# Splits of operands to twelve bits, queued at other places: query rows, output weights, and the first layer's change of rows

## The chip, the cores and the metric

The kernel runs on one core of one Trainium2 chip, in one launch. The metric is the device time of an execution in microseconds (us), as the median of several runs. TensorE is called PE here, VectorE DVE, ScalarE ACT, GpSimd POOL, and SyncE, which issues most DMAs, SP.

## The reference

A graph network on 1024 nodes of width 512: layer norm and relu of the input, batch norm, a graph convolution, four layers of cross-attention and a gated feed-forward net, a second graph convolution, and two additions of the input. Cut to what this change touches, each of the four layers computes:

```python
def _attn(xf, cond, Wq, Wk, Wv, Wo):            # xf 1024x512, cond 16x256x512
    xb = xf.reshape(BS, n // BS, d)             # 16 groups of 64 rows
    q = (xb @ Wq).reshape(BS, -1, H, DH)
    k = (cond @ Wk).reshape(BS, -1, H, DH)
    v = (cond @ Wv).reshape(BS, -1, H, DH)
    att = jnp.einsum('bnhd,bmhd->bhnm', q, k) * DH ** (-0.5)
    w = jax.nn.softmax(att, axis=-1)
    o = jnp.einsum('bhnm,bmhd->bnhd', w, v).reshape(BS, -1, H * DH)
    return (o @ Wo).reshape(n, d)
for i in range(L):                              # L = 4
    h = h + _attn(_ln(h, ln2_w[i], ln2_b[i]), cond, Wq[i], Wk[i], Wv[i], Wo[i])
    u = _ln(h, ln3_w[i], ln3_b[i]) @ geglu_w[i] + geglu_b[i]
    ...
```

## The kernel before

The rows of `h` lie in SBUF as eight blocks of 128 rows; two batches of `cond` make one of eight groups `g`. The large products run on PE in a reduced fp32 form (`twelve_bits`): both operands are split into a high part (ACT, a scaled copy), a low part (DVE) and a third part, a sum or difference of the two (POOL for left operands, DVE for the rows and the output weights). A product is then three sets of four matmuls. The class `Twelve` holds one such product: `begin` multiplies the high parts and the low parts into a PSUM bank and lets ACT scale the bank in place (line 377); `end` multiplies the third parts onto it and copies the bank out. `staggered` runs a list of them so that the `begin` of one stands ahead of the `end` of the one before, with a callback beside each.

A layer begins with the query phase. The rows of `h` are normalised (`xn`), transposed on PE (`tr_ln`, line 201), scaled and shifted out of PSUM into `ln2T` by DVE (line 812) and ACT (line 814) in turn, and split: `Rows.high` makes the high part `bh_ln` on ACT (line 1252), `Rows.rest` makes the low part `bl_ln` (line 1257) and the third part `bs_ln` (line 1260) on DVE. `QueryWeights` does the like for `Wq` (`ah_wq`, `al_wq`, `as_wq`). The queries of the first four blocks are multiplied while the other four are turned and split; then those of the second half follow. In layers 1 to 3 the query phase stands behind the keys and values of group 0; in layer 0 most of these have been made during the graph convolution.

Then come the scores of group 0 and the loop over the groups: the keys of the next group, the weighing of the values of this one (`po`), the scores and the softmax of the next group (DVE line 834 takes the maxima `nmax`, ACT line 839 eight exponentials `pr`, DVE line 844 divides), the values of the next group, and the product with the output weights `wo`. `out_parts` splits `wo` once a layer, in group 0: `oh` on ACT (line 915), `ol` and `os` on DVE (lines 918 and 921). `split_cond` splits the `cond` of the group after next (`ah_c`, `al_c`, `as_c`; lines 314, 315 and 320). In groups 1 and 2 `base_of` prepares two blocks of the final sum from the input `x`: a load `x_again`, an ACT operation `again` (line 1526), two DVE additions (1528 and 1529), and a store (1530).

What order the instructions of an engine get is decided by the scheduler of the language, except where the code pins it: `pin` keeps the written order, `in_order(engine)` chains all that is recorded inside it on that engine, `waiting_for` adds a wait. PE's large products are pinned. In layers 1 to 3 ACT and parts of DVE are chained in the query phase; in layer 0 they are not. `base_of` and the copies around the softmax are nowhere pinned.

Of the kernel before, what the change touches and what calls it, by code (L numbers as in the profile page):

```python
# [25 lines left out]
def gnn_kernel(  # L26
# [114 lines left out]
    def rsqrt(var, name, eps=0.0):  # L141


        k = var.shape[1]

        def t(n, dtype=F32):
            return small.tile([P, k], dtype, tag=f"rs_{n}{k}", name=f"{n}_{name}",
                              bufs=4 if k == 1 or n == "y" else 2)

        v = t("v")  # L150
        rsqrt.first = nc.vector.tensor_scalar(v, var, float(eps), None, OP.add)
        y = t("y")
        nc.vector.tensor_scalar(y.bitcast(I32), v.bitcast(I32), -0.5, RSQRT_SEED, OP.mult, OP.add)
        for i in range(3):
            a = t("a")
            nc.vector.scalar_tensor_tensor(a, y, -0.5, v, OP.mult, OP.mult)
            b = t("b")
            nc.vector.tensor_tensor(b, a, y, OP.mult)
            y2 = t("y")
            nc.vector.scalar_tensor_tensor(y2, b, 1.5, y, OP.add, OP.mult)  # L160
            y = y2
        return y

# [138 lines left out]
    def twelve_bits(t):  # L302
        return t.bitcast(F32R)
# [605 lines left out]
    def out_parts(l, wo):  # L909

        high = four_wide(f"oh_{l}")
        low = slots_of(2, f"ol_{l}")
        third = [acc_tile(f"os_{l}_{c}") for c in range(HP)]
        for k in range(2):
            nc.scalar.mul(twelve_bits(high)[:, 2 * k:2 * k + 2, :], wo[k], INWARD / TINY)
        for k in range(2):
            of = high[:, 2 * k:2 * k + 2, :]
            nc.vector.scalar_tensor_tensor(twelve_bits(low[k]), wo[k], 1.0 / TINY, of, OP.mult,
                                           OP.subtract)
            for i in range(2):  # L920
                out_parts.last = nc.vector.scalar_tensor_tensor(
                    twelve_bits(third[2 * k + i]), of[:, i, :], -TINY, low[k][:, i, :], OP.mult,
                    OP.add)
        return ([high[:, c, :] for c in range(HP)], [low[c // 2][:, c % 2, :] for c in range(HP)],
                third)

    def order7(blk, s1, s2, s4):

# [315 lines left out]
    class Rows:  # L1244
# [6 lines left out]
                part.append(slot(f"b{n}_{self.n}_{i}"))  # L1251
            nc.scalar.mul(twelve_bits(self.parts[0][i]), self.x[i], INWARD / TINY)

        def rest(self, i):
            (h, l, s), x = (t[i] for t in self.parts), self.x[i]
            for k in range(2):
                nc.vector.scalar_tensor_tensor(twelve_bits(l)[:, k, :], x[:, k, :], 1.0 / TINY,
                                               h[:, k, :], OP.mult, OP.subtract)
            for k in range(2):
                Rows.last = nc.vector.scalar_tensor_tensor(  # L1260
                    twelve_bits(s)[:, k, :], h[:, k, :], -TINY, l[:, k, :], OP.mult, OP.add)

    class QueryWeights:

# [139 lines left out]
    for l in range(L):  # L1404
# [3 lines left out]
        if l:  # L1408
            units = keys(l, 0, wk, by=(0, 0)) + values(l, 0, wv, by=(0, 0))
            units[0].to()  # L1410
        else:
            scale_first(1, deviations(mv_first[1], "ln2_0_4"))
            for i in range(2):
                wq.high(i)
                with waiting_for(scale_first.last, mybir.EngineType.Pool):
                    wq.rest(i)
            kTs[0], vs[0], kTs[1] = (begun[n] for n in ("k0", "v0", "k1"))
            units = keys(0, 0, wk, 2) + values(0, 0, wv, 1)
# [14 lines left out]
        def split_first(i):  # L1433
            first_rows.high(i)
            with in_order(mybir.EngineType.DVE):
                first_rows.rest(i)

        def turn_more(*blocks):
            with in_order(mybir.EngineType.DVE) if l else nullcontext():
                turn_first(l, blocks, ((1, 1), (0, 0)))  # L1440

        def split_more(i):
            nonlocal more_rows
            if not i:
                more_rows = Rows(l, 1, lnT[1])
            more_rows.high(i)
            with in_order(mybir.EngineType.DVE):
                more_rows.rest(i)

        def split_wq(i):  # L1450
            wq.high(i)
# [6 lines left out]
        if l:  # L1458
            with in_order(mybir.EngineType.Activation):
# [4 lines left out]
                                  7: lambda: to_scale[0](0, 1)})  # L1464
                staggered_queries(0, first_rows, {
                    0: lambda: (to_scale[0](2, 3), turn_more(*half[1][:2])),
                    1: lambda: turn_more(*half[1][2:]),
                    2: lambda: split_more(0), 3: lambda: split_more(1)})
                to_scale.clear()
        else:  # L1470
            staggered(units, {2: turn_some, 3: lambda: split_first(0), 4: lambda: split_first(1)})
            fetch_cond(2)
            staggered_queries(0, first_rows, {0: lambda: turn_more(*range(4, 8)),
                                              2: lambda: split_more(0), 3: lambda: split_more(1)})
        split_cond(l, 1)
        staggered_queries(1, more_rows, {})
        qT = [qTs.pop(i) for i in range(2)]
# [73 lines left out]
        for g in range(NG - 1):  # L1551
# [6 lines left out]
            if g == NG - 2:  # L1558
                with waiting_for(scores.last, mybir.EngineType.Pool):
                    left = geglu_weights(l, 0, *raw)  # L1560
            if not g:
                wo = out_parts(l, wo)
            if g in (1, 2):
                fetch_x(2 * l + g - 1)
            k = keys(l, g + 1, wk, 1 if l == 0 and g == 0 else 0)
            for i, u in enumerate(k):
# [3 lines left out]
                        end()  # L1570
                if i > 1:
                    k[i - 2].end()
            k[-2].end()
            v = values(l, g + 1, wv)
            with in_order(mybir.EngineType.DVE) if g == NG - 2 else nullcontext():
                oT = mix(l, g, probs, vs.pop(g), (
# [375 lines left out]
```

## Time and profile before

| | |
|---|---|
| median of 3 runs | 2312.1 us (2311.81 to 2313.15) |
| the profiled execution's own time | 2312.45 us |
| its span, from the first to the last instruction | 2310.6 us |
| PE busy | 2282.0 us, 99% of the span |
| DVE, ACT, POOL busy | 1688.6, 1136.0, 646.2 us |
| granted TensorE clock | 1.000 |

The span is what the trace covers; 1.85 us of the execution's own time lie outside it. A row of the timeline gives the start, the duration, the engine, the line, and the operation with its output and inputs; rows that follow each other in one group are merged, and their count stands behind an x. In brackets stands the idle time of that engine ahead of the row, and what ended it. Matmuls overlap in PE's pipeline, so that the time from start to start tells more than the durations.

### The profile page before, as it was taken

Reading aid. Unit: us, or ns where it says so; the run is one execution under the profiler, and the core shown is the slowest. Engines: PE = TensorE matmul, PEld = TensorE weight load, DVE = VectorE, ACT = ScalarE, POOL = GpSimd, SP = SyncE. Lnnn points to the kernel's source line nnn. Section 1 sums busy time; section 2 is a strip of 40 time slices with the busy share of each in tenths; the row PEclk is TensorE's granted clock in tenths of the full one; section 3 lists DMA queues with packets and bytes.
Section 4 is the critical chain, followed back from the end, with each engine's and each line's share of the span. In section 5 each row is a group of like instructions: output and inputs, shape, how many; then the busy total and the mean of one; then the engine's idle time right before and its main releaser. Section 6 shows DMA issues by size and latency. Waiting matters only on the chain. (4 is left out here: it accounts for less than half of the span.)

```text
span 2310.6 us, 33998 instructions
## 1 busy us (share of the span) xinstructions
PE 2282.0 (99%) x12416; PEld 1742.7 (75%) x12416; DVE 1688.6 (73%) x3092; ACT 1136.0 (49%) x2183; POOL 646.2 (28%) x575
## 2 busy tenths in 40 slices
PE   8999999999999999999999999999999999999999
PEld 5677887577887888477887888577787888667787
DVE  9886557888976556978887554988887555888964
ACT  7555445455365445455356444555337444545420
POOL 1112223274021224165021222266022113156111
PEclk9999999999999999999999999999999999999999
DMA  7042220245412101144522111133531111033550
GB/s 214 11 142 72 66 80 17 73 128 162 167 46 74 55 20 37 46 130 133 176 90 74 37 37 37 33 112 118 186 128 54 43 50 38 12 111 125 173 192 37
DMA packets 144110, 204.39 MB, mean 88 GB/s; under 512 B 11240, under 2 KB 68912, under 8 KB 143936
## 3 DMA queue, kind: packets, MB, share of 16 engines
q1 hardware_dynamic: 141840, 196.72, 26.3%
q0 software_dynamic: 1376, 4.30, 0.5%
q8 instruction: 102, 1.67, 0.3%
q10 hardware_dynamic: 720, 1.11, 0.1%
q14 instruction: 72, 0.59, 0.1%
HBM read 151.75 MB, written 50.34 MB: 87 GB/s over the span
## 5 line engine op out<-in xcount | busy, mean ns | idle before, releaser
L320 POOL TENSOR_TENSOR as_c<-ah_c,al_c 128x512 fp32r<-128x512 f32 x128 | 196.8, 1564 | 916.3 <-DVE al_c L315 497.2
L1104 ACT ACTIVATE g<-g 128x512 f32<-128x512 f32 x192 | 112.8, 588 | 193.5 <-PE g L1090 193.5
L377 ACT ACTIVATE k<-k 128x512 f32<-128x512 f32 x125 | 72.2, 584 | 201.8 <-PE k L366 201.8
L1234 PE MATMUL fy<-bh_wff,ah_f 128*128 128x512 f32 x512 | 159.2, 392 | 0.0
L1234 PE MATMUL fx<-bs_wff,as_f 128*128 128x512 f32 x512 | 157.7, 389 | 0.5 <-DVE as_f L317 0.5
L1234 PE MATMUL fy<-bl_wff,al_f 128*128 128x512 f32 x512 | 157.9, 389 | 0.0
L314 ACT ACTIVATE ah_f<-fr 128x1024 fp32r<-128x1024 f32 x64 | 67.5, 1060 | 173.6 <-PE fy L1234 112.1
L382 DVE COPY kT<-k 128x512 f32<-128x512 f32 x54 | 37.2, 688 | 156.8 <-PE k L366 156.8
L366 PE MATMUL v<-bs_wv,as_c 128*128 128x512 f32 x508 | 137.0, 392 | 4.9 <-ACT v L377 4.9
L366 PE MATMUL v<-bh_wv,ah_c 128*128 128x512 f32 x508 | 140.8, 399 | 0.0
L366 PE MATMUL v<-bl_wv,al_c 128*128 128x512 f32 x508 | 136.5, 390 | 0.0
L1090 PE MATMUL g<-gr,gsa 128*128 128x512 f32 x384 | 136.2, 436 | 0.0
L839 ACT ACTIVATE pr<-sc,nmax 128x256 f32<-128x256 f32 x256 | 118.0, 474 | 35.1 <-DVE nmax L834 34.5
L366 PE MATMUL k<-ah_c,bh_wk 128*128 128x512 f32 x500 | 135.1, 392 | 0.0
L366 PE MATMUL k<-as_c,bs_wk 128*128 128x512 f32 x500 | 132.3, 395 | 1.9 <-ACT k L377 1.9
L366 PE MATMUL k<-al_c,bl_wk 128*128 128x512 f32 x500 | 133.8, 389 | 0.0
L1036 POOL TENSOR_TENSOR gsa<-gha,gla 128x512 fp32r<-128x512 f32 x88 | 112.3, 1297 | 66.7 <-DVE gla L1032 66.7
L377 ACT ACTIVATE v<-v 128x512 f32<-128x512 f32 x127 | 75.0, 591 | 110.5 <-PE v L366 108.3
L1090 PE MATMUL g<-gr,gha 128*128 128x512 f32 x384 | 120.7, 395 | 0.0
L1090 PE MATMUL g<-gl,gla 128*128 128x512 f32 x384 | 118.6, 390 | 0.0
L366 PEld LDWEIGHTS v<-bs_wv,as_c 128*128 128x128 f32 x508 | 93.2, 188 | 30.0 <-ACT v L377 8.1
L366 PEld LDWEIGHTS v<-bh_wv,ah_c 128*128 128x128 f32 x508 | 92.6, 188 | 27.9 <-issue 9.2
(321 smaller groups left out, 5620.6 us busy)
## 6 DMA issues: line engine op xcount, KB each, us to landing
f_dram<-fT SPq DMA_DIRECT2D x128, 256.0 KB, 2.0
fr<-f_dram SPq DMA_DIRECT2D x64, 512.0 KB, 4.5
ct<-cond_dram SPq DMA_DIRECT2D x48, 512.0 KB, 4.6
wff<-in_L_gnn_ffo_w_dram SPq DMA_DIRECT2D x32, 512.0 KB, 5.9
gxb<-in_L_gnn_geglu_w_dram SPq DMA_DIRECT2D x96, 128.0 KB, 2.4
gxa<-in_L_gnn_geglu_w_dram SPq DMA_DIRECT2D x96, 128.0 KB, 2.6
cond<-in_L_gnn_cond_dram SPq DMA_DIRECT2D x32, 256.0 KB, 3.7
cond_dram<-ct SPq DMA_DIRECT2D x16, 512.0 KB, 3.3
```

Of the source, the lines that this page charges most:

```text
L314: nc.scalar.mul(twelve_bits(h), x, INWARD * TINY)
L320: nc.gpsimd.tensor_tensor(twelve_bits(s)[:, k, :], h[:, k, :], l[:, k, :], OP.subtract)
L366: pin(nc.tensor.matmul(self.bank, twelve_bits(left[k // 2])[:, k % 2, self.c * P:(self.c + 1) * P], twelve_bits(right[k // 2])[:, k % 2, : ...
L377: nc.scalar.mul(self.bank, self.bank, 1.0 + TINY)
L382: nc.vector.tensor_copy(self.to(), self.bank)
L839: nc.scalar.activation(pr3[:, a, :], ps3[:, a, :], AF.Exp, bias=nmax[:, a:a + 1], accum_out=tot[:, a:a + 1])
L1036: split_left.last = pin(t.tensor_tensor(s_at, h_at, l_at, OP.subtract))
L1090: pin(nc.tensor.matmul(to, self.part(i, which)[:, k, :], self.rights[i][which].bitcast(F32R)[:, k, :], start=start and k == 0, stop=stop a ...
L1104: pin(nc.scalar.mul(to, to, 1.0 + TINY))
L1234: pin(nc.tensor.matmul(to, twelve_bits(left[which][0])[:, k, b * P:(b + 1) * P], twelve_bits(right[which])[:, k, :], start=u == 0 and whic ...
```

## The change

Four things are changed.

In the query phase of layers 1 to 3, `split_more` becomes `begin_more` and `finish_more`: the high parts of the second half's rows are queued on ACT one callback sooner, each ahead of a scaling of a query bank instead of behind it, and the low and third parts follow one callback later. `Rows.rest` becomes `low` and `third`.

`out_parts` becomes a generator: it hands out its tiles at once, and its pieces (two on ACT, two on DVE) are recorded one per key block of group 0, instead of all ahead of the keys.

In layer 0 the query phase is chained on ACT and DVE in the order as written. There the second half's normalised rows (`scale_first(1)`) are made behind the third parts of the first half, the turning of the second half stands behind the second query block, and POOL's third part of `Wq` waits for the last step of the reciprocal root (`rsqrt.last`) instead of for the normalised rows. The fetch of the third group's `cond` is written behind both.

The names of lines shift: 1252, 1257, 1260 become 1254, 1259, 1265; 915, 918, 921 become 917, 921, 924; 1526 to 1530 become 1540 to 1544.

```diff
             y2 = t("y")
-            nc.vector.scalar_tensor_tensor(y2, b, 1.5, y, OP.add, OP.mult)
+            rsqrt.last = nc.vector.scalar_tensor_tensor(y2, b, 1.5, y, OP.add, OP.mult)
...
         third = [acc_tile(f"os_{l}_{c}") for c in range(HP)]
+        yield ([high[:, c, :] for c in range(HP)], [low[c // 2][:, c % 2, :] for c in range(HP)],
+               third)
         for k in range(2):
             nc.scalar.mul(twelve_bits(high)[:, 2 * k:2 * k + 2, :], wo[k], INWARD / TINY)
+            yield
         for k in range(2):
             of = high[:, 2 * k:2 * k + 2, :]
...
                     OP.add)
-        return ([high[:, c, :] for c in range(HP)], [low[c // 2][:, c % 2, :] for c in range(HP)],
-                third)
+            yield
...
-        def rest(self, i):
-            (h, l, s), x = (t[i] for t in self.parts), self.x[i]
+        def low(self, i):
+            (h, l, _), x = (t[i] for t in self.parts), self.x[i]
             for k in range(2):
                 nc.vector.scalar_tensor_tensor(twelve_bits(l)[:, k, :], x[:, k, :], 1.0 / TINY,
                                                h[:, k, :], OP.mult, OP.subtract)
+
+        def third(self, i):
+            h, l, s = (t[i] for t in self.parts)
             for k in range(2):
...
-            scale_first(1, deviations(mv_first[1], "ln2_0_4"))
+            root = deviations(mv_first[1], "ln2_0_4")
             for i in range(2):
                 wq.high(i)
-                with waiting_for(scale_first.last, mybir.EngineType.Pool):
+                with waiting_for(rsqrt.last, mybir.EngineType.Pool):
                     wq.rest(i)
...
         def split_first(i):
             first_rows.high(i)
             with in_order(mybir.EngineType.DVE):
-                first_rows.rest(i)
+                first_rows.low(i)
+                if l:
+                    first_rows.third(i)
...
-        def split_more(i):
+        def begin_more():
             nonlocal more_rows
-            if not i:
-                more_rows = Rows(l, 1, lnT[1])
-            more_rows.high(i)
+            more_rows = Rows(l, 1, lnT[1])
+
+        def finish_more(i):
             with in_order(mybir.EngineType.DVE):
-                more_rows.rest(i)
+                more_rows.low(i)
+                more_rows.third(i)
...
-                    1: lambda: turn_more(*half[1][2:]),
-                    2: lambda: split_more(0), 3: lambda: split_more(1)})
+                    1: lambda: (turn_more(*half[1][2:]), begin_more(), more_rows.high(0)),
+                    2: lambda: (finish_more(0), more_rows.high(1)),
+                    3: lambda: finish_more(1)})
                 to_scale.clear()
         else:
-            staggered(units, {2: turn_some, 3: lambda: split_first(0), 4: lambda: split_first(1)})
+            with in_order(mybir.EngineType.Activation), in_order(mybir.EngineType.DVE):
+                staggered(units, {2: turn_some, 3: lambda: split_first(0),
+                                  4: lambda: (split_first(1), first_rows.third(0),
+                                              first_rows.third(1), scale_first(1, root))})
+                staggered_queries(0, first_rows, {
+                    1: lambda: (turn_more(*range(4, 8)), begin_more(), more_rows.high(0)),
+                    2: lambda: (finish_more(0), more_rows.high(1)),
+                    3: lambda: finish_more(1)})
             fetch_cond(2)
-            staggered_queries(0, first_rows, {0: lambda: turn_more(*range(4, 8)),
-                                              2: lambda: split_more(0), 3: lambda: split_more(1)})
...
-            if not g:
-                wo = out_parts(l, wo)
+            wo_flow = out_parts(l, wo) if not g else iter(())
+            wo = next(wo_flow, wo)
...
                 if i > 1:
                     k[i - 2].end()
+                next(wo_flow, None)
             k[-2].end()
+            for _ in wo_flow:
+                pass
```

How the scheduler then sets the rows, at three places. First ACT in the query phase of layer 1, where the second half's rows `ln2T_1` have just been turned; `q_0_2`, `q_0_3` are banks that are scaled, `qT` are copies out. Before:

```order
L814 ACTIVATE ln2T_1_1_20383<-tr_ln_1_7_20587,cols 128x128 x2
L377 ACTIVATE q_0_2_20596<-q_0_2_20596 128x512
L384 COPY qT_0_0_20575<-q_0_1_20561 128x512
L1252 ACTIVATE bh_ln_1_1_0_20611<-ln2T_1_0_20382 128x1024
L377 ACTIVATE q_0_3_20619<-q_0_3_20619 128x512
L1252 ACTIVATE bh_ln_1_1_1_20634<-ln2T_1_1_20383 128x1024
L384 COPY qT_0_1_20576<-q_0_3_20619 128x512
```

The same place in the changed kernel:

```order
L814 ACTIVATE ln2T_1_1_20383<-tr_ln_1_7_20587,cols 128x128 x2
L1254 ACTIVATE bh_ln_1_1_0_20596<-ln2T_1_0_20382 128x1024
L377 ACTIVATE q_0_2_20600<-q_0_2_20600 128x512
L384 COPY qT_0_0_20575<-q_0_1_20561 128x512
L1254 ACTIVATE bh_ln_1_1_1_20619<-ln2T_1_1_20383 128x1024
L377 ACTIVATE q_0_3_20623<-q_0_3_20623 128x512
L384 COPY qT_0_1_20576<-q_0_3_20623 128x512
```

Each `bh_ln` has moved ahead of the scaling that it followed. Layers 2 and 3 read alike. In group 0 of these layers ACT's two `oh`, which stood together behind the exponentials and ahead of the scalings of `k_1_0`, `k_1_1` and `k_1_2`, now stand between them.

Second, DVE and ACT around the softmax of group 1 in layer 1, which the diff doesn't touch. DVE before (`x_again`, `again`: the final sum's first block; `al_c_2`: the split of the `cond` of group 2):

```order
L315 SCALAR_TENSOR_TENSOR al_c_2_0_21007<-ah_c_2_0_21005,ct_2_0_20727 128x1024
L382 COPY kT_1_1_20841<-k_1_3_20843 128x512
L1528 TENSOR_TENSOR x_again_21088<-x_again_21088,bias_out_21086 128x512
L315 SCALAR_TENSOR_TENSOR al_c_2_1_21008<-ah_c_2_1_21006,ct_2_1_20728 128x1024
L1529 TENSOR_TENSOR x_again_21088<-x_again_21088,again_21294 128x512
L834 TENSOR_REDUCE nmax_1_0_20963<-sc_1_0_20943 128x2
```

DVE in the changed kernel:

```order
L382 COPY kT_1_1_20835<-k_1_3_20840 128x512
L315 SCALAR_TENSOR_TENSOR al_c_2_0_21007<-ah_c_2_0_21005,ct_2_0_20727 128x1024
L1542 TENSOR_TENSOR x_again_21088<-x_again_21088,bias_out_21086 128x512
L1543 TENSOR_TENSOR x_again_21088<-x_again_21088,again_21294 128x512
L315 SCALAR_TENSOR_TENSOR al_c_2_1_21008<-ah_c_2_1_21006,ct_2_1_20728 128x1024
L834 TENSOR_REDUCE nmax_1_0_20963<-sc_1_0_20943 128x2
```

ACT a little later, before (`v_1_1` is the bank of values that PE waits to go on with; `again_21586` belongs to the final sum's second block):

```order
L839 ACTIVATE pr_1_1_20975,tot_1_1_20976<-sc_1_1_20944,nmax_1_1_20973 128x256 x2
L839 ACTIVATE pr_1_2_20985,tot_1_2_20986<-sc_1_2_20945,nmax_1_2_20983 128x256 x2
L839 ACTIVATE pr_1_3_20995,tot_1_3_20996<-sc_1_3_20946,nmax_1_3_20993 128x256 x2
L377 ACTIVATE v_1_1_21023<-v_1_1_21023 128x512
L384 COPY v_1_0_21037<-v_1_0_20897 128x512
L1526 ACTIVATE again_21586<-x_again_21380,x_shift,x_root 128x512
```

ACT in the changed kernel:

```order
L839 ACTIVATE pr_1_1_20975,tot_1_1_20976<-sc_1_1_20944,nmax_1_1_20973 128x256 x2
L1540 ACTIVATE again_21586<-x_again_21380,x_shift,x_root 128x512
L839 ACTIVATE pr_1_2_20985,tot_1_2_20986<-sc_1_2_20945,nmax_1_2_20983 128x256 x2
L839 ACTIVATE pr_1_3_20995,tot_1_3_20996<-sc_1_3_20946,nmax_1_3_20993 128x256 x2
L377 ACTIVATE v_1_1_21023<-v_1_1_21023 128x512
L384 COPY v_1_0_21037<-v_1_0_20897 128x512
```

On DVE the addition of `again` has moved ahead of `al_c_2_1`, and on ACT the second `again` has moved in between the exponentials; with it, on SP, the store of the first block and the load of the second stand ahead of the two loads of `ct_3` instead of behind them. Layers 2 and 3 read alike. In layer 0 the second `again` moves the other way: it stood between `pr_1_1` and `pr_1_2`, and now stands behind the scaling of `v_1_1`.

Third, DVE in layer 0, from the end of the reciprocal root (`y_ln_0_4`) to the splits of the first half's rows. Before:

```order
L160 SCALAR_TENSOR_TENSOR y_ln_0_4_15311<-b_ln_0_4_15309,y_ln_0_4_15305 128x4
L189 TENSOR_SCALAR xn_ln_0_4_0_15313<-hall,mv_first_15019,y_ln_0_4_15311 128x512
...
L1277 SCALAR_TENSOR_TENSOR al_wq_1_15327<-ah_wq_15290,wq_1_15279 128x1024
L382 COPY k_begun_455<-k_0_3_15343 128x512
L812 TENSOR_SCALAR ln2T_0_0_15021<-tr_ln_0_0_15373,cols 128x128
L812 TENSOR_SCALAR ln2T_0_0_15021<-tr_ln_0_1_15382,cols 128x128
L812 TENSOR_SCALAR ln2T_0_0_15021<-tr_ln_0_2_15391,cols 128x128
L812 TENSOR_SCALAR ln2T_0_1_15022<-tr_ln_0_0_15373,cols 128x128
```

In the changed kernel:

```order
L160 SCALAR_TENSOR_TENSOR y_ln_0_4_15311<-b_ln_0_4_15309,y_ln_0_4_15305 128x4
L1282 SCALAR_TENSOR_TENSOR al_wq_1_15319<-ah_wq_15290,wq_1_15279 128x1024
L382 COPY k_begun_455<-k_0_3_15335 128x512
L812 TENSOR_SCALAR ln2T_0_0_15021<-tr_ln_0_0_15365,cols 128x128
L812 TENSOR_SCALAR ln2T_0_1_15022<-tr_ln_0_0_15365,cols 128x128
L812 TENSOR_SCALAR ln2T_0_0_15021<-tr_ln_0_1_15374,cols 128x128
L812 TENSOR_SCALAR ln2T_0_1_15022<-tr_ln_0_1_15374,cols 128x128
```

The four `xn_ln_0_4` have left this place (they stand behind the eight `bl_ln` and `bs_ln` now), and the `ln2T` go block by block instead of half by half; ACT's `ln2T` do the same, and ACT's scaling of the bank `v_0_2`, which stood ahead of the last of them, stands behind them all. On each block the two engines write the same two tiles and wait for each other: DVE's first for ACT's first, ACT's second for DVE's first, DVE's second for ACT's second.

More of the change, by code (lines that the diff above doesn't have):

```diff
@@ L1258, in rest @@
                                                h[:, k, :], OP.mult, OP.subtract)
+        def third(self, i):
+            h, l, s = (t[i] for t in self.parts)
             for k in range(2):
-                Rows.last = nc.vector.scalar_tensor_tensor(
-                    twelve_bits(s)[:, k, :], h[:, k, :], -TINY, l[:, k, :], OP.mult, OP.add)
+                nc.vector.scalar_tensor_tensor(twelve_bits(s)[:, k, :], h[:, k, :], -TINY,
+                                               l[:, k, :], OP.mult, OP.add)
     class QueryWeights:
```

## Prediction

> **What bounds the kernel now.** I read the page first, then the waits of PE, then the timeline around each of those waits.
>
> ```profile
> span 2310.6 us, 33998 instructions
> PE 2282.0 (99%) x12416; PEld 1742.7 (75%) x12416; DVE 1688.6 (73%) x3092; ACT 1136.0 (49%) x2183; POOL 646.2 (28%) x575
> ```
>
> PE is busy 99% of the span, and the diff leaves its matmuls as they are. So the edit can only take away or add moments in which PE stands still for another engine. The three rows of PE's waits which belong to the places changed:
>
> ```profile
> PE v L366 <- ACT v L377: 4.9, 6, 2.5
> PE k L366 <- ACT k L377: 1.9, 3, 0.6
> PE q L366 <- DVE bl_ln L1257: 1.7, 4, 0.9
> ```
>
> Columns are us in total, times, longest. Together 8.5 us, 0.4% of the span: that caps a gain at these waits, apart from what a listed wait leaves out. It leaves some out, since ends of matmuls are modelled; I therefore count from start to start. The query phase of layer 1:
>
> ```profile
> 684.81 1.50 ACT L814 ACTIVATE ln2T<-tr_ln,cols 128x128 f32<-128x128 f32 x4 [0.62 <-PE tr_ln L201]
> 687.36 1.10 PE L366 MATMUL q<-bh_ln,ah_wq 128*128 128x512 f32 x4
> 688.04 1.06 ACT L1252 ACTIVATE bh_ln<-ln2T 128x1024 fp32r<-128x1024 f32 x1
> 689.21 2.03 PE L366 MATMUL q<-bs_ln,as_wq 128*128 128x512 f32 x8
> 691.08 1.10 PE L366 MATMUL q<-bh_ln,ah_wq 128*128 128x512 f32 x4
> 692.16 1.28 DVE L1257 SCALAR_TENSOR_TENSOR bl_ln<-ln2T,bh_ln 128x512 fp32r<-128x512 f32 x2
> 693.83 1.10 PE L366 MATMUL q<-bh_ln,ah_wq 128*128 128x512 f32 x4
> ```
>
> An undisturbed `begin` takes 689.21 - 687.36 = 1.85 us. The first one of the second half takes 693.83 - 691.08 = 2.75, so 0.90 is lost per layer. The keys of group 1, in the same layer:
>
> ```profile
> 708.79 2.04 ACT L915 ACTIVATE oh<-wo 128x1024 fp32r<-128x1024 f32 x2
> 708.86 1.07 PE L366 MATMUL k<-ah_c,bh_wk 128*128 128x512 f32 x4
> 711.46 1.16 PE L366 MATMUL k<-as_c,bs_wk 128*128 128x512 f32 x4 [0.62 <-ACT k L377]
> ```
>
> Here 711.46 - 708.86 - 1.85 = 0.75 is lost, behind the two `oh`.
>
> **Layers 1 to 3: query rows.** `bh_ln_1_0` now stands ahead of a scaling. Its input is there at 684.81 + 1.50 = 686.31, against its start at 688.04. The second `bh_ln` likewise gets ahead of one scaling, and DVE's `bl_ln` at 692.16 comes over 1 us sooner; 0.9 is enough, so the whole 0.90 goes: -0.90 a layer. Next late would be the scaling of `q_0_3`, which now stands behind a `bh_ln` of 1.06; it has the slack of the `end` ahead of it (689.21, eight matmuls of two banks in 2.03) and I cost it at nothing, at most 0.5 if that cover is too short.
>
> **Layers 1 to 3: output weights.** The scaling of `k_1_0` can follow the exponentials at 708.79, where `oh` stood, so PE's 0.75 goes. But PE's next wait there is for the softmax of group 1, which hangs on DVE and POOL:
>
> ```profile
> 720.02 2.96 POOL L320 TENSOR_TENSOR as_c<-ah_c,al_c 128x512 fp32r<-128x512 f32 x2 [17.71 <-issue]
> 720.40 1.45 DVE L1528 TENSOR_TENSOR x_again<-x_again,bias_out 128x512 f32<-128x512 f32 x1
> 721.77 2.29 DVE L315 SCALAR_TENSOR_TENSOR al_c<-ah_c,ct 128x1024 fp32r<-128x1024 f32 x1
> 723.99 0.68 DVE L1529 TENSOR_TENSOR x_again<-x_again,again 128x512 f32<-128x512 f32 x1
> 724.59 1.28 DVE L834 TENSOR_REDUCE nmax<-sc 128x2 f32<-128x512 f32 x2
> 728.32 0.47 ACT L839 ACTIVATE pr<-sc,nmax 128x256 f32<-128x256 f32 x1 [0.16 <-DVE nmax L834]
> 729.24 0.59 ACT L377 ACTIVATE v<-v 128x512 f32<-128x512 f32 x1
> 729.88 1.20 PE L366 MATMUL v<-bs_wv,as_c 128*128 128x512 f32 x4 [0.45 <-ACT v L377]
> 730.23 0.82 ACT L1526 ACTIVATE again<-x_again,x_shift,x_root 128x512 f32<-128x512 f32 x1
> ```
>
> DVE's `x_again` takes 1.45 at 720.40 and 0.68 at 723.99, the same shape and kind. At 720.40 POOL's `as_c` runs, at 723.99 it does not: the two engines take turns. I read from this that DVE's additions and `al_c` and POOL's two `as_c` (2.96) form one line, so that their new order hardly moves its end. That `al_c_2_0` now stands behind the copy of `k_1_3`, whose input PE delivers 0.75 sooner, costs one copy of about 0.7. So `nmax`, which ends the line at 724.59, stays within 0.1 of this clock, and the 0.75 turns into waiting in front of `v`. Behind `nmax` the second `again` now stands between the exponentials: +0.82 at its row's duration, about +0.72 as ACT's rows overlap by some 0.1 (two `oh` take 2.04 where two of 1.06 would make 2.12), less the 0.16 that ACT idles at 728.32 anyway: the scaling of `v_1_1` at 729.24 comes 0.6 later, and PE's `v` at 729.88 with it. Per layer -0.90 + 0.6 = -0.3, over three layers **-0.9**.
>
> The Trainium skill, "SBUF — State Buffer", section "SBUF: two separate sides", says why: DVE, with two inputs from SBUF, and POOL share a port pair, which whoever starts first holds for the whole instruction. By it the line is the plain sum of its pieces in any order, and the sum above stands; if the two did not hinder each other, DVE's three instructions alone would end some 2.4 us sooner a layer. The row of 1.45 agrees with the rule.
>
> **Layer 0: values.** The same place:
>
> ```profile
> 181.98 1.27 DVE L834 TENSOR_REDUCE nmax<-sc 128x2 f32<-128x512 f32 x2
> 185.47 0.82 ACT L1526 ACTIVATE again<-x_again,x_shift,x_root 128x512 f32<-128x512 f32 x1 [0.85 <-DMA x_again<-in_x_dram]
> 187.99 0.60 ACT L377 ACTIVATE v<-v 128x512 f32<-128x512 f32 x1
> 188.64 1.21 PE L366 MATMUL v<-bs_wv,as_c 128*128 128x512 f32 x4 [2.46 <-ACT v L377]
> ```
>
> Here `again` leaves the exponentials, and with it ACT's wait of 0.85 for its load: -0.72 - 0.85 = -1.57, the chain from `nmax` to 187.99 taken as it is. Against that, `x_again`'s second addition and `al_c_2_1` now go in DVE's other order ahead of `nmax` (181.98), each behind one of POOL's pieces: 0 to +0.9. I take the later end, nearest to the row at 720.40: **-0.7**, with ends at -1.6 and 0.
>
> **Layer 0: rows.**
>
> ```profile
> 127.22 1.92 DVE L189 TENSOR_SCALAR xn_ln<-hall,mv_first,y_ln 128x512 f32<-128x512 f32 x4
> 130.78 2.39 DVE L812 TENSOR_SCALAR ln2T<-tr_ln,cols 128x128 f32<-128x128 f32 x7
> 131.22 1.50 ACT L814 ACTIVATE ln2T<-tr_ln,cols 128x128 f32<-128x128 f32 x4 [2.90 <-DVE ln2T L812]
> 133.21 0.46 ACT L814 ACTIVATE ln2T<-tr_ln,cols 128x128 f32<-128x128 f32 x1
> 133.70 0.41 DVE L812 TENSOR_SCALAR ln2T<-tr_ln,cols 128x128 f32<-128x128 f32 x1
> 138.02 1.27 DVE L1257 SCALAR_TENSOR_TENSOR bl_ln<-ln2T,bh_ln 128x512 fp32r<-128x512 f32 x2
> 140.43 2.63 DVE L812 TENSOR_SCALAR ln2T<-tr_ln,cols 128x128 f32<-128x128 f32 x8
> 148.80 2.03 PE L366 MATMUL q<-bs_ln,as_wq 128*128 128x512 f32 x8
> 149.00 0.58 ACT L377 ACTIVATE q<-q 128x512 f32<-128x512 f32 x1 [1.21 <-PE q L366]
> ```
>
> The four `xn` (1.92) leave the front, so the first `ln2T` starts at 130.78 - 1.92 = 128.86. The blocks then cost more: DVE to ACT takes 131.22 - 130.78 = 0.44, ACT's step (1.50 - 0.46) / 3 = 0.35, ACT to DVE 133.70 - 133.21 = 0.49, and 1.28 for a block written in turn. Four blocks take 5.1 where they took 133.70 - 130.78 + 0.41 = 3.3. What the front gains, the turns nearly give back: `bl_ln` of the second tile, at 138.02 before, comes about 1.0 sooner, at 137.05.
>
> But the `xn` must be made somewhere. From 137.05: three pairs of splits at 1.2 (1.27 less their overlap) end at 140.65, the four `xn` at 142.57, two copies out (0.6 each, estimated as half of such a pair) at 143.8; six of the eight `ln2T`, at 2.63 / 8 = 0.33, let the first `bh_ln` of the second half begin at 145.8. ACT then does that (1.06), a scaling (0.58), a copy of like size and the second `bh_ln` (1.06): overlaps of 0.1 taken off each, that is 2.9, and the scaling of `q_0_3` begins at 148.7 to 148.9 and ends by 149.45. PE's last third product of the first half, at 148.80 + 0.91 = 149.71 before (half of eight matmuls' 1.85), follows at about 149.5: **-0.2**. Ends: PE alone would be there at 148.6 (-1.1); and if POOL, which may start on `as_wq` sooner now, holds up `al_wq` by one of its pieces (1.27, as a DVE pair), all comes that much later (+1.1).
>
> **Sum** for the profiled execution of 2312.45: -0.9 - 0.7 - 0.2 = -1.8, that is 2310.65. Its time stands 0.35 above the median of 2312.1, from which I forecast 2310.3.
>
> **The rivals.** *DVE keeps its turn* (faster). The two additions stand together now; if POOL does not get in between them, `nmax` loses one piece of POOL from its line, 2.96 / 2 less an overlap, about 1.2 us, in each of layers 1 to 3, and 0.9 in layer 0: -1.8 - 3.6 - 0.9 = -6.3, 2305.8. For it speaks that three DVE instructions now stand ready in a row, so that it needs no luck but DVE's being first each time; against it that at 721.77 `al_c` followed 720.40 directly and still took 2.29, a piece of POOL longer than a pair of splits.
>
> *The load of `x_again` comes late* (slower). In layers 1 to 3 the second `again` needs a load that SP issues behind a store of the block before it, and it now stands ahead of PE's scaling on ACT.
>
> ```profile
> x_again<-in_x_dram SPq DMA_DIRECT2D x1, 256.0 KB, 8.8
> x_again<-in_x_dram SPq DMA_DIRECT2D x1, 256.0 KB, 4.7
> x_again<-in_x_dram SPq DMA_DIRECT2D x1, 256.0 KB, 2.7
> ```
>
> These are its landings, in us from issue, in windows at 700, 724 and 180 us. The addition that the store waits for ends near 722.4 by an estimate: from 720.0 two additions of 0.6 and a piece of POOL, (2.96 - 0.5) / 2 = 1.2. With 0.4 for the store's issue, the load leaves at 722.8. It is wanted two exponentials of 0.47 and the 0.16 ahead of 728.32, at 727.2. It decides from a landing of 4.3. With 4.7 it costs 0.4 a layer; with 8.8 it costs 4.5 x 3 = 13.5, 2323.8. Against it: the loads of `ct_3`, which at 724 ran ahead of it, are issued behind it now, as nothing was at 180. If a landing is shared with them as at 700, it is slower by over 0.2% from 6.5 us on. By the Trainium skill, "DMA: Bandwidth & Descriptors", section "Queues, rings and completion order", descriptors of one ring start in order, so that later loads would not hold this one up; by it the landing would be near 2.7 and the cost nothing. No row here shows that.
>
> *Layer 0 does not do what it says* (no gain): +1.1 in its rows, and `nmax` there 0.7 later still: 2312.3, no change.
>
> **How the numbers follow.** The bound of 0.2%, 4.6 us, is about what a measurement of this kernel can tell from no change. My forecast has 0.42, DVE's turn 0.32, the late load 0.16, layer 0's failure 0.10. Forecast and failure lie within the bound: 0.52. DVE's turn gives -6.3; with two of its places missing (-3.9) it would fall within the bound, for which I move 0.02: faster 0.30, same 0.54, and slower 0.16 for the load, whose smaller costs are counted with the forecast. The range goes from DVE's turn with PE's own end of layer 0's rows (-1.1 in place of -0.2), 2304.9, to a landing of 5.3 in three layers, 2310.3 + 3.0 = 2313.3, with +1.3 in layer 0's rows: 2314.6.
>
> **What would show it.** Right: no wait of PE for `bl_ln` and `k` in layers 1 to 3; `nmax_1_0` in layer 1 at 723.7 (724.59 less the 0.9 of the queries); the longest wait for `v` in layer 0 under 2.5, and in layers 1 to 3 about 0.45 + 0.75 + 0.6 = 1.8. DVE's turn would show as an `x_again` addition of 0.68 in place of 1.45 ahead of POOL's `as_c`. A bracket with a DMA ahead of ACT's `again` among the exponentials shows the late load. Wrong altogether: if PE's waits elsewhere grow, or DVE's `ln2T` in layer 0 take no turns.

## The result and the profile after

The changed kernel takes 2308.52 us (median of 19 runs), the kernel before 2312.91 (19 runs beside it): 4.4 us less, a ratio of 0.9982, 95% interval 0.9975 to 0.9990. The forecast was -1.8 us and 2310.3, with a range of 2304.9 to 2314.6. The profiled execution went from 2312.45 to 2308.50 us; I account for its span.

First the page of the changed kernel, then its waits of PE (us in total, times, longest):

```profile
span 2306.7 us, 34003 instructions
PE 2279.3 (99%) x12416; PEld 1742.9 (76%) x12416; DVE 1686.9 (73%) x3092; ACT 1135.5 (49%) x2183; POOL 648.8 (28%) x575
```

```profile
PE v L366 <- ACT v L377: 7.4, 6, 1.7
PE q L366 <- ACT q L377: 0.4, 1, 0.4
PE k L366 <- ACT k L377: 0.2, 1, 0.2
```

The waits for `bl_ln` (1.7 before) are gone and those for `k` nearly so, while the wait for `v` has grown from 4.9 to 7.4. Adding up such rows would nearly cancel the gain; the starts of PE's rows tell where the time went. For each landmark, a row of PE but for the first, its start before and how much it moved:

| landmark | before | after less before |
|---|---|---|
| last step of the reciprocal root on DVE, layer 0 | 127.02 | -0.38 |
| first scores of layer 0 | 163.59 | -0.67 |
| scores of group 1 | 179.46 | -0.62 |
| scores of group 2 | 214.47 | -1.43 |
| turning of rows, layer 1 | 667.38 | -1.46 |
| scores of group 0, layer 1 | 703.17 | -2.37 |
| scores of group 1, layer 1 | 722.72 | -3.32 |
| scores of group 2, layer 1 | 753.94 | -2.27 |
| turning, layer 2 | 1199.73 | -2.27 |
| turning, layer 3 | 1732.05 | -2.99 |
| turning for the feed-forward net, layer 3 | 1976.65 | -3.91 |

Read it as steps. In layer 1 the query phase gives 0.91, the keys of group 1 0.95, and the values of group 1 take 1.05 back. Layer 0 gives 0.29 in its rows and 0.81 in its values. The first 0.38 stands ahead of everything changed.

The timeline of the query phase and the keys in layer 1:

```profile
684.76 1.07 ACT L1254 ACTIVATE bh_ln<-ln2T 128x1024 fp32r<-128x1024 f32 x1
685.92 1.10 PE L366 MATMUL q<-bh_ln,ah_wq 128*128 128x512 f32 x4
687.77 2.03 PE L366 MATMUL q<-bs_ln,as_wq 128*128 128x512 f32 x8
689.48 1.28 DVE L1259 SCALAR_TENSOR_TENSOR bl_ln<-ln2T,bh_ln 128x512 fp32r<-128x512 f32 x2
689.63 1.09 PE L366 MATMUL q<-bh_ln,ah_wq 128*128 128x512 f32 x4
691.47 1.10 PE L366 MATMUL q<-bh_ln,ah_wq 128*128 128x512 f32 x4
...
706.45 1.07 PE L366 MATMUL k<-ah_c,bh_wk 128*128 128x512 f32 x4
708.26 1.07 PE L366 MATMUL k<-as_c,bs_wk 128*128 128x512 f32 x4
```

The first `begin` of the second half takes 691.47 - 689.63 = 1.84 (2.75 before): `bl_ln` of its second tile starts at 689.48, ahead of the `begin` itself. Group 1's keys take 708.26 - 706.45 = 1.81 (2.60 before). The softmax of group 1 in the same layer:

```profile
717.63 3.30 POOL L320 TENSOR_TENSOR as_c<-ah_c,al_c 128x512 fp32r<-128x512 f32 x2 [18.38 <-PE v L366]
717.41 0.69 DVE L1542 TENSOR_TENSOR x_again<-x_again,bias_out 128x512 f32<-128x512 f32 x1
718.13 1.66 DVE L1543 TENSOR_TENSOR x_again<-x_again,again 128x512 f32<-128x512 f32 x1
719.71 2.29 DVE L315 SCALAR_TENSOR_TENSOR al_c<-ah_c,ct 128x1024 fp32r<-128x1024 f32 x1
721.93 1.27 DVE L834 TENSOR_REDUCE nmax<-sc 128x2 f32<-128x512 f32 x2
722.64 0.47 ACT L839 ACTIVATE pr<-sc,nmax 128x256 f32<-128x256 f32 x1 [2.52 <-DVE nmax L834]
724.45 0.83 ACT L1540 ACTIVATE again<-x_again,x_shift,x_root 128x512 f32<-128x512 f32 x1
726.96 0.63 ACT L377 ACTIVATE v<-v 128x512 f32<-128x512 f32 x1
727.64 1.20 PE L366 MATMUL v<-bs_wv,as_c 128*128 128x512 f32 x4 [1.52 <-ACT v L377]
```

The line is the one forecast: the first addition undisturbed (0.69), the second behind one piece of POOL (1.66), `al_c` behind the other (2.29), then `nmax`; layers 2 and 3 have the same durations. PE's wait for `v`, 0.45 before, is 1.52; no bracket with a DMA stands ahead of `again`. The landing of its load, from the DMA view of 719 to 729 us:

```profile
x_again<-in_x_dram SPq DMA_DIRECT2D x1, 256.0 KB, 2.8
```

### The profile page after: what moved, and what is told of

It reads as the page before. It is cut to its first block, busy times and chain, and to the rows that moved or that the text cites. A ratio compares the mean times of both kernels' runs of the same rounds, so it can differ in the third digit from the quotient of the medians.

```text
span 2306.7 us, 34003 instructions
## 1 busy us (share of the span) xinstructions
PE 2279.3 (99%) x12416; PEld 1742.9 (76%) x12416; DVE 1686.9 (73%) x3092; ACT 1135.5 (49%) x2183; POOL 648.8 (28%) x575
## 3 DMA queue, kind: packets, MB, share of 16 engines
q10 hardware_dynamic: 720, 1.11, 0.1%
```

## Experiments

The times are medians of 4 to 10 executions (POOL's run has one), and the ratios (with a 95% interval) are against the kernel before, run beside the experiment. Where an experiment is compared by stage, it is by the starts of the same landmarks. A stage of layers 1 to 3 repeats from run to run within 0.1 us; layer 0's beginning does not, which is taken up below.

**The query rows alone.** The kernel before, in layers 1 to 3 only:

```diff
-                    1: lambda: turn_more(*half[1][2:]),
-                    2: lambda: split_more(0), 3: lambda: split_more(1)})
+                    1: lambda: (turn_more(*half[1][2:]), begin_more(), more_rows.high(0)),
+                    2: lambda: (finish_more(0), more_rows.high(1)),
+                    3: lambda: finish_more(1)})
```

> The kernel before with only the new order of the query rows in layers 1 to 3. Theory (each stretch pays by itself): PE's `begin` of the second half in the query phase takes 1.85 instead of 2.75 in each layer, and nothing later takes it back, since the keys and values behind it have not changed: -0.9 x 3 = -2.7 us. Rival (what is gained here waits again in front of the keys or of the softmax): the wait for `k` behind the two `oh` or the wait for `v` grows by the same 0.9 and the sum is 0.

2308.81 us (ratio 0.9985, 0.9975 to 0.9994). From the turning of one layer to the next layer norm, the offset against before goes from 0.60 to -0.36, from -0.38 to -1.34, and from -1.36 to -2.33: 0.96 a layer, -2.9 in all, and nothing takes it back. The rival falls. The medians say more, -4.2 (2312.99 for the kernel before beside it), for a reason that the last section gives: among executions whose mean granted clock was 1.000 they are 2308.70 against 2311.79, -3.1.

**The output weights alone.** The kernel before with the generator:

```diff
-            if not g:
-                wo = out_parts(l, wo)
+            wo_flow = out_parts(l, wo) if not g else iter(())
+            wo = next(wo_flow, wo)
...
+                next(wo_flow, None)
```

> The kernel before with only the output weights' parts handed out one per key block. Theory (the gain of the keys turns into waiting): in layers 1 to 3 the scores of group 1 begin 0.95 sooner and PE waits some 1.0 longer for `v`, so that these layers end at 0 to +0.1 each; layer 0, where the second `again` leaves the exponentials, gains 0.8. Sum -0.8 to -0.5 us. Rival (the keys' gain is kept, and what the changed kernel gained is mostly this): -0.8 a layer in layers 1 to 3, -3.2 us in all.

2311.16 us (ratio 0.9994, 0.9984 to 1.0003). In layers 1 to 3 group 1's scores begin 0.95 sooner each time and group 2's are back to where they were: the layers end at +0.05, +0.06 and +0.05. Layer 0's values gain 0.81 (-0.73 to -1.54). The waits of PE say the same:

```profile
PE v L366 <- ACT v L377: 7.1, 6, 1.7
PE q L366 <- DVE bl_ln L1259: 1.8, 4, 0.9
```

The wait for `k` is gone and stands under `v` now, 7.1 against 4.9. The theory holds: the keys' gain is turned into waiting, and this part pays in layer 0 only.

**Layer 0's query phase alone.** The kernel before with the chained order in layer 0:

```diff
-            staggered(units, {2: turn_some, 3: lambda: split_first(0), 4: lambda: split_first(1)})
+            with in_order(mybir.EngineType.Activation), in_order(mybir.EngineType.DVE):
+                staggered(units, {2: turn_some, 3: lambda: split_first(0),
+                                  4: lambda: (split_first(1), first_rows.third(0),
+                                              first_rows.third(1), scale_first(1, root))})
...
```

> The kernel before with only layer 0's query phase chained in the written order. Theory: the first query of the second half begins 0.66 sooner, as in the changed kernel, and nothing else moves: -0.66 us, within what a median can tell but plain in the start of the scores. Rival (layer 0's gain in the rows needs the other parts, or is taken back by the softmax of group 1): 0 from the values of group 1 on.

2311.67 us (ratio 0.9997, 0.9987 to 1.0007): no difference that a median shows. The trace tells why a start in clock time misleads. The last step of the root on DVE, from which this order goes its own way, and the first scores:

```profile
126.61 0.16 DVE L160 SCALAR_TENSOR_TENSOR y_ln<-b_ln,y_ln 128x4 f32<-128x4 f32 x1
163.20 1.96 PE L827 MATMUL sc<-k_begun,qT 64*64 64x256 f32 x32
```

From one to the other it takes 36.59 here. With the old order it takes 163.59 - 127.02 = 36.57 in the kernel before, and 36.60 and 36.56 in the two runs above; with the new one 36.28 in the changed kernel, and 36.27 and 36.26 in two of the runs below. (The next run has 37.17, with PE at half its clock for 3.4 us in this stretch; the last section comes back to that.) So the new order gives 0.3 us or nothing. Where it gave nothing (here, and in one run below with 36.62), the second half of `Wq` had landed late: ACT waited for it, with PE's scaling of `k` behind. In this run that was

```profile
122.18 1.06 ACT L1278 ACTIVATE ah_wq<-wq 128x1024 fp32r<-128x1024 f32 x1 [2.53 <-DMA wq<-in_L_gnn_Wq_dram]
```

against 1.26 in the changed kernel (2.50 in the later run with 36.62). The expected -0.66 was read off the clock, which had 0.38 of another cause in it.

**The final sum's additions behind the softmax.** The changed kernel with

```diff
             if g in (1, 2):
-                base_of(2 * l + g - 1)
+                with tc.issue_after(scores.last.ins):
+                    base_of(2 * l + g - 1)
```

> The changed kernel, where the additions and with them the second `again` of the final sum's blocks are queued behind the softmax of their own group, so that neither stands ahead of or within the softmax of group 1. Theory (PE's wait for `v` hangs on the line of DVE and POOL and on the `again` between the exponentials): `nmax` of group 1 about 1.4 sooner, the exponentials 0.45 shorter, the wait for `v` of 1.7 in each of the four layers gone: -1.7 x 4 = -6.7 us against the changed kernel. Rival (PE's `v` waits for the scores or POOL's pieces alone): the wait stays above 1 and the gain is under -2.5. A third: the additions delay the later groups instead, and the time is the same or longer.

2304.63 us (ratio 0.9966, 0.9954 to 0.9979). By the medians it is 3.9 under the changed kernel, where 6.7 was expected. Against the changed kernel the values of group 1 give 1.11, 1.16 and 1.15 us in layers 1 to 3 (+0.17 to -0.94, and so on), not 1.7, and PE's wait for `v` there is 0.39 instead of 1.52. DVE in layer 1:

```profile
716.45 1.22 DVE L315 SCALAR_TENSOR_TENSOR al_c<-ah_c,ct 128x1024 fp32r<-128x1024 f32 x1
719.29 2.10 DVE L315 SCALAR_TENSOR_TENSOR al_c<-ah_c,ct 128x1024 fp32r<-128x1024 f32 x1 [1.63 <-ACT ah_c L314]
721.32 1.28 DVE L834 TENSOR_REDUCE nmax<-sc 128x2 f32<-128x512 f32 x2
```

The additions are out of the way, and the second `al_c` is late next: it waits 1.63 for ACT's high part, which stands behind the scaling of `v_1_0` as in the changed kernel, and then takes 2.10 beside POOL's piece. The place was right, the size was not.

**The next `cond` behind the softmax as well.** On top of the last one, in group 0:

```diff
+            with tc.issue_after(scores.max.ins) if not g else nullcontext():
-            split_cond(l, g + 2)
+                split_cond(l, g + 2)
```

where `scores.max` is the softmax's last `nmax`.

> The changed kernel, where the final sum's additions stand behind their group's softmax and, in group 0, both low parts of the next `cond` (and with them POOL's pieces) are queued on DVE behind the maxima of group 1. Theory: with the line of DVE and POOL gone from in front of it, `nmax` of group 1 follows its scores, near 720.6 in layer 1 against 721.3 with the additions alone moved; PE's wait for `v` is under 0.2 in layers 1 to 3, that is -1.0 to -1.2 a layer below the additions' own part of the gain in the changed kernel: 2302 to 2303 us. Rival (the parts moved are wanted by the keys of group 2, which then wait): a new wait for `k` of 1 us or more a layer and 2305 us or more.

2302.49 us (ratio 0.9953, 0.9936 to 0.9969): the fastest kernel of this study, 6.0 us under the changed one by the medians. DVE and PE in layer 1, then the waits of PE:

```profile
718.97 1.29 DVE L834 TENSOR_REDUCE nmax<-sc 128x2 f32<-128x512 f32 x2 [4.17 <-PE sc L827]
723.63 0.59 ACT L377 ACTIVATE v<-v 128x512 f32<-128x512 f32 x1
724.40 1.09 PE L366 MATMUL v<-bs_wv,as_c 128*128 128x512 f32 x4
```

```profile
PE v L366 <- ACT v L377: 1.0, 2, 0.7
PE k L366 <- ACT k L377: 0.4, 1, 0.4
```

`nmax` now waits for its scores alone, PE's `v` stands without a bracket, and the wait for `v` fell from 7.4 to 1.0. The layers 1 to 3 gain 1.53, 1.58 and 1.46 against the changed kernel, 0.3 to 0.4 more than by the additions alone, and layer 0's values of group 1 gain 1.23; no wait of the size feared appeared at the keys of group 2. So this is where the keys' 0.95 a layer had gone.

**The second `again` alone.** The changed kernel, where in layers 1 to 3 that block is queued behind the scaling of `v_1_1`:

```diff
             if g in (1, 2):
-                base_of(2 * l + g - 1)
+                with tc.issue_after(v_first.ins) if l and g == 2 else nullcontext():
+                    base_of(2 * l + g - 1)
```

`v_first` is the scaling of `v_1_1`, written in group 0.

> The changed kernel, where in layers 1 to 3 the second `again` is queued on ACT behind the scaling of `v_1_1`, where it stood before. It prices that move by itself. Theory: the scaling of `v_1_1` comes 0.4 to 0.55 sooner behind the first exponential, and PE with it: -1.2 to -1.6 us in all. Rival (the exponentials wait for the maxima anyway, and the move was free): 0.

2307.75 us (ratio 0.9975, 0.9966 to 0.9985). The values of group 1 give 0.35, 0.36 and 0.33 a layer, 1.0 in all: neither free nor the 0.4 to 0.55 expected. ACT shows why:

```profile
722.47 0.48 ACT L839 ACTIVATE pr<-sc,nmax 128x256 f32<-128x256 f32 x1 [2.52 <-DVE nmax L834]
725.56 0.47 ACT L839 ACTIVATE pr<-sc,nmax 128x256 f32<-128x256 f32 x1 [0.23 <-DVE nmax L834]
726.48 0.59 ACT L377 ACTIVATE v<-v 128x512 f32<-128x512 f32 x1
```

Without `again` ACT idles 0.23 for the last `nmax`, which `again` filled. From the first exponential to the scaling it is 4.01 here and 726.96 - 722.64 = 4.32 with it.

**POOL behind the softmax.** The changed kernel with POOL's pieces held back:

```diff
+            with waiting_for(scores.max, mybir.EngineType.Pool) if not g else nullcontext():
-            split_cond(l, g + 2)
+                split_cond(l, g + 2)
```

> The changed kernel, where POOL's pieces for the `cond` of group 2 wait for the maxima of group 1; the scheduler then also puts ACT's second high part of that `cond` ahead of the scaling of `v_1_1` (+0.95) and DVE's second low part behind the softmax. Theory (DVE and POOL take turns): the second addition of `x_again` right behind the first takes 0.69 instead of 1.66, with nothing else changed in front of it, and `nmax` comes 1.4 or more sooner. Rival (the addition is long because it waits for its operand `again` or for its own predecessor): it stays near 1.6.

One execution of 2313.48 us, so only its rows are used. DVE in layer 1:

```profile
719.32 0.69 DVE L1542 TENSOR_TENSOR x_again<-x_again,bias_out 128x512 f32<-128x512 f32 x1
720.04 0.69 DVE L1543 TENSOR_TENSOR x_again<-x_again,again 128x512 f32<-128x512 f32 x1
722.44 1.29 DVE L834 TENSOR_REDUCE nmax<-sc 128x2 f32<-128x512 f32 x2 [1.71 <-PE sc L827]
```

The second addition takes 0.69 where it took 1.66, with the same work ahead of it on DVE, and `nmax` begins 1.13 behind the first scores instead of 2.53, the 1.4 expected. So it was POOL's piece that held the addition up, as the forecast read from 1.45 against 0.68, and not its operands. The layers lose time all the same, as PE's waits show:

```profile
PE oy L899 <- DVE ol L888: 3.0, 3, 1.0
```

PE waits for DVE's `ol` in each of three layers, 1.0 each, and the values of group 1 lose 0.85, 0.87 and 0.89 there.

**Layer 0's first rows, whole blocks in turn.** The changed kernel with

```diff
-                turn_first(0, range(4))
+                turn_first(0, range(4), ((1, 1), (0, 0)))
```

> The changed kernel, where the first half's rows in layer 0 are shifted and scaled whole blocks in turn, two by DVE and two by ACT, instead of every block by both. Theory (the turns on each block cost the front of layer 0's query phase): no row of `ln2T` waits 0.5 for the other engine, eight of them take 1.5 to 1.8 instead of 5.1, the wait of 0.9 for `v` at 133 us goes, and the first query of the second half begins 1 to 2 us sooner against the start of the turning: -1 to -2 us. Rival (POOL's third part of the query weights or DVE's copies set that end): under -0.4.

2307.60 us (ratio 0.9974, 0.9964 to 0.9983), 0.9 under the changed kernel, while the profiled execution (2308.95) was not faster. DVE and ACT:

```profile
128.94 2.63 DVE L812 TENSOR_SCALAR ln2T<-tr_ln,cols 128x128 f32<-128x128 f32 x8
134.55 0.58 ACT L377 ACTIVATE v<-v 128x512 f32<-128x512 f32 x1 [1.07 <-PE v L366]
```

The eight `ln2T` take 2.63 and none waits, but ACT then waits for PE, whose turning began 1.68 later in this run than in the changed kernel's: ACT had waited 2.44 for the second half of `Wq`. From the root to the scores it is 36.15, against 36.28. One more run, with this and the softmax first together:

> The changed kernel with the softmax of group 1 put first (as in the run of that name) and layer 0's first rows turned whole blocks in turn. Theory: the turns on each block were not what ended layer 0's rows, since PE's bank for ACT and DVE's copies and `xn` stand behind them, so that from the end of the reciprocal root on DVE to the first scores the time stays at 36.0 to 36.3 us against 36.27, and the whole at 2301.5 to 2302.8. Rival (in the run with whole blocks the late landing of the query weights hid a gain of 1 to 2 us): 35.3 or less there, and about 2301 in all.

2302.68 us (ratio 0.9956, 0.9939 to 0.9973), the same as without it. From the root to the scores 163.17 - 127.56 = 35.61, between the two numbers expected, and again with PE's turning late (127.94, 1.58 after the changed kernel's; here PE had run at half its clock from 85.8 us, while ACT's wait for `Wq` was 1.13). Compared with the runs in which `Wq` landed alike, whole blocks in turn give 0.4 us with the late landing (36.15 against 36.59 and 36.62) and 0.65 with the early one (35.61 against 36.26 to 36.28). So the turns on each block seem to cost layer 0 about half a microsecond, by one run of each kind; the rival's 1 to 2 us were not hidden there.

## Why the forecast was right, and where its sizes were off

**Query rows, -0.90 a layer: right.** 0.88 to 0.94 in the changed kernel, 0.96 alone by the end of the layer, and the scaling of `q_0_3` cost nothing, as assumed.

**Keys, -0.75 a layer, turned into waiting for `v`: right in kind.** The keys gave 0.95: the stretch that was counted went from 2.60 to 1.81, which is 0.79; the product behind the wait, from its start to the next one's, went from 1.00 to 0.91; and 0.07 is spread over other rows. The output weights alone left layers 1 to 3 at +0.05.

**Values, +1.35 a layer (0.75 + 0.6): too large.** It was 1.05. This is the term that was mis-sized: with the keys' 0.95 it leaves +0.10 a layer where +0.6 was forecast, so that a layer gave -0.79, -0.70 and -0.92 instead of -0.3, a difference of 1.5 us over three layers. Two parts of it were off. `again` was charged 0.56, rounded to 0.6, and cost 0.33 to 0.36, because it partly fills ACT's wait for the last `nmax`: I took off the 0.16 of one row, and the run without it has 0.23 there and rows that follow closer. And `nmax` was put at the same clock as before. Less the 1.46 by which layer 1 began sooner and the 0.91 of its query phase, 724.59 becomes 722.22; it started at 721.93, 0.3 sooner. DVE's line began with the copy of `k_1_3`, for which PE was 0.95 ahead, not 0.75, which accounts for 0.2 of it.

**Layer 0's values, -0.7: right in size, partly by luck.** It was 0.81. Without `again` the stretch from `nmax` to the scaling of `v` went from 187.99 - 181.98 = 6.01 to 186.57 - 182.25 = 4.32, 1.69 less where 1.57 was forecast. And `nmax` came 0.89 later against the scores, as the end that was taken had it (+0.9), but not for the reason given. In the changed kernel:

```profile
177.49 0.80 ACT L1540 ACTIVATE again<-x_again,x_shift,x_root 128x512 f32<-128x512 f32 x1
178.32 1.18 DVE L1542 TENSOR_TENSOR x_again<-x_again,bias_out 128x512 f32<-128x512 f32 x1 [0.79 <-ACT again L1540]
181.11 1.21 DVE L315 SCALAR_TENSOR_TENSOR al_c<-ah_c,ct 128x1024 fp32r<-128x1024 f32 x1
186.57 0.64 ACT L377 ACTIVATE v<-v 128x512 f32<-128x512 f32 x1
```

The forecast had `al_c` held up by POOL, and it takes 1.21, undisturbed. What is late is the first addition, by 1.15 against the scores: it waits 0.79 for ACT's first `again`, which ran at 175.44 before, ahead of a scaling of `v`, and now stands behind one. From there to `nmax` the line is even 0.26 shorter than before. The forecast did not see this move.

**Layer 0's rows, -0.2: right as far as it can be seen.** 0.3 or nothing, from the end of the root on. The forecast's single steps there were good, the turns on each block among them: the first `ln2T` was expected at 128.86 and stood at 128.46, the scaling of `q_0_3` at 148.7 to 148.9 and stood at 148.33, in an execution that was 0.38 early.

**The sum.** -3.9 by the trace: 0.38 stood ahead of the change, 1.5 was the term above, 1.8 the forecast, and 0.2 the rest. So the change itself is worth 3.5 us here, twice the forecast: the way and the places were right, the size was not. The 4.4 of the medians has more in it, since the profiled execution of before (2312.45) lay 0.46 under its own later median (2312.91). Among executions with a mean granted clock of 1.000 the medians are 2308.38 (13 of the changed kernel) and 2311.79 (11 of the kernel before, beside the first experiments), which is 3.4.

**The rivals.** DVE did not keep its turn. The sign named for it, an addition of 0.68 in place of 1.45, did appear on the first addition (0.69), but the second took 1.66 and `al_c` 2.29: POOL got in between, and the line was no shorter. The load of `x_again` was not late: it landed in 2.8, under the 4.3 from which it decides (by the forecast's own 727.2 - 722.8 it is 4.4), with the two loads of `ct_3` issued right behind it. That is near the 2.7 of the row at 180 us. By the Trainium skill's rule ("DMA: Bandwidth & Descriptors", section "Queues, rings and completion order"), that the descriptors of one ring are taken in order, the loads behind it were not expected to hold it up; the trace agrees with it here. Layer 0 gained.

## What to carry to other kernels

When an engine is late twice in a row, removing the first wait moves the time into the second: look for what ends last one stage on, and price the two together. Here the output weights' part of the edit earned nothing in three layers until the work that no one was waiting for yet (the additions, the parts of the next `cond`) was queued behind the softmax that PE did wait for. Compare two traces by the starts of the same instruction on the busiest engine, from an anchor behind everything that varies from run to run, and not by summing listed waits.

## What the runs showed of the hardware

In four of the eleven traces the granted clock of PE fell to half for 3.4 us, once in the execution. In three of them this was in layer 0 (the query rows alone, the additions moved, POOL held back), behind waits for `v` of 2.33, of 1.33 and 0.24, and of 2.04; in the run with both orders it was ahead of layer 0, at 85.8 us, behind a wait of 1.97. In the run with the query rows alone; timeline and windows (start and end, length, busy time and count of each engine, then the granted clock, the DMA share and GB/s):

```profile
187.84 2.08 PE L366 MATMUL v<-bs_wv,as_c 128*128 128x512 f32 x4 [2.33 <-ACT v L377]
189.71 1.75 PE L899 MATMUL oy<-oh,oh 128*128 128x512 f32 x4
```

```profile
186.00:188.00 2.00, 0.16 (x1) 0.16 (x1) 1.75 (x7) 2.00 (x8) 0.00 (x0) 0.93 0.00 0
188.00:190.00 2.00, 2.00 (x5) 1.62 (x6) 1.76 (x5) 0.79 (x2) 0.00 (x0) 0.50 0.90 280
190.00:191.50 1.50, 1.50 (x5) 1.16 (x5) 0.64 (x1) 0.00 (x0) 0.00 (x0) 0.62 0.91 317
```

Half the clock lasts 0.28 + 2.00 + 1.14 = 3.42 us by these three windows. Four matmuls take 2.08 instead of 1.21; group 2's scores begin 0.65 later than before, where group 1's had been 0.68 sooner, so 1.3 is lost. In the kernel before, a wait of 2.46 at the same place left the clock at 1.00. So a short wait can cost more than itself, and not every time.

This also sorts the executions. The four traces with a fall have a mean granted clock of 0.999, the other seven 1.000. Of the 27 executions of the kernel before beside the first experiments, 11 have 1.000 (2311.42 to 2312.27 us), 13 have 0.999 (2312.80 to 2314.00) and 3 have 0.998 (2314.12 to 2314.41), while 13 of the 19 of the changed kernel have 1.000. So medians of the two compare different numbers of falls. The run of the output weights, which shortens the wait of 2.46, had a fall in none of its 10 executions, and those of the query rows and of layer 0, which leave it, in 3 and 4 of 10; that the shorter wait makes falls rarer is only suggested by this.

Part of what decides it can be read from the traces. In all four the stretch at full clock ahead of the fall is a whole multiple of the fall's 3.413 us (51, 35, 51 and 21 times), so that time seems cut into windows of this length. In the window just ahead of the fall PE was busy for 35%, 54%, 40% and 42%. In the kernel before, the wait of 2.46 lay across the border of two such windows, with 63% and 65%. The share alone does not settle it: two windows with 48%, in the run with the softmax first and in that of whole blocks, were followed by no fall. The Trainium skill ("TensorE: Matmul & The Clock Gate", section "Part 1: The HAM clock gate (the "warmup" mystery)") has the clock halved behind an idle window of some 3.4 us, where the windows run freely; the halving, the length and the free run agree with these traces, while PE was not idle for the whole window here.
